# A graph kernel's step re-ordered: transposes side by side, block sums one step later, node stages in a PSUM bank of their own

## The chip, the cores and the metric

The kernel runs on one NeuronCore of a Trainium2 chip. The engines named here are TensorE (PE, with its weight loads as PEld), VectorE (DVE), ScalarE (ACT), GpSimd (POOL) and SyncE (SP, which only issues transfers). Each engine works through its own queue in the order of the program. The metric is the device time of one launch in microseconds; less is better.

## What is computed

Two layers of a graph network on 6,250 nodes with 256 features and 106,250 edges, sorted by the node they point to, all in float32. In the reference, cut to what matters:

```python
# layer 0
msg = relu(x[src] + edge_attr)
agg = segment_sum(msg, dst, num_segments=N)
h = x + (x + agg)
f = gelu(bn1(h) @ W1.T + b1) @ W2.T + b2
x1 = layernorm(x + bn2(h + f))
# layer 1
m = gelu((x1[src] + edge_attr) @ W1m + b1m) @ W2m + b2m
agg = segment_sum(m, dst, num_segments=N) / maximum(deg, 1)
u = gelu(agg @ W1u + b1u) @ W2u + b2u
out = layernorm(x1 + layer_norm(x1 + u, gamma, beta))
```

## The kernel before

Edges come in tiles of 128, eight tiles to a *span*: 831 tiles make V = 104 spans, the last of 7 tiles with 10 edges in its last. A span has two groups of four tiles (`g` = 0 and 1), and a group two pairs (`q` = 0 and 2). Nodes come in 25 blocks of 256 rows, the last (block 24) of 106. There is one pass over all spans for each layer (`step_0` and `step_1`).

The edges being sorted, the targets of a span lie in a window of some 160 nodes, and those of two neighbouring tiles in 32 slots. So the segment sum is two products with 0/1 matrices: `into_slots` (L855) sums a span's rows into 4 x 32 slots with one-hots that `one_hots` makes (L833); the result is copied out by ScalarE (L861); `into_blocks` (L879) adds the slots into the accumulator of one or two node blocks, with a mask of the span's window made by `slot_nodes` (L842), or a wider one where a block is begun (L873). In pass 0 a third product (L886) adds up the degrees.

A span's rows of `x[src]` (or, in pass 1, of `proj[src]`, which is x1 @ W1m + b1m) are fetched by `gather` (L772): one indirect transfer a tile, 128 rows of 1 KB, issued by GpSimd into one of five ring buffers. A ring is free again when `into_slots` of the span five earlier has read it. Loads of edge features (L760, L1158) are issued by SyncE three steps ahead into eight buffers.

The product edge_attr @ W1m is needed in pass 1, but half of it (group 0) is made in pass 0, stored to memory (`zst`, L1041) and loaded in pass 1, so that TensorE has like work in both. For a pair of tiles, `turned` transposes the features (four transposes, L785, into one PSUM bank of the pool eaP), ScalarE copies the result out (L790), and `product` multiplies with W1m (L798). Where no product is needed, `lifted` has ScalarE copy the features to PSUM (L809). `add_to_gathered` (L816, VectorE) adds the PSUM tile onto the ring, and `activated` (L824, ScalarE) applies Relu or Gelu over four tiles.

Step v gathers span v, adds and activates span u = v - 1, and sums span w = v - 2 into slots and blocks. When a block's last span has been summed, a Python generator (`nodes_0` or `nodes_1`) does the node work in stages, one a step, with `advance`; the stages lie in the list `running`. `nodes_0` has five: scale and copy the accumulator (L924, L929); W1 and Gelu (L935, L940); W2, residual and the first layer norm, up to the store of x1 (L948 to L962); transposes of x1 (L970, L973); the product with W1m and the store of proj (L979, L987). `nodes_1` has five as well: mean (L1086 to L1090); two with half of the first product each (L1100, L1105, L1109); the second product with the inner layer norm (L1115 to L1136); the outer one and the store (L1141). `normalized` makes statistics (L898, L899) on VectorE, a square root on ScalarE (L900, which loads another function table than Gelu) and the scaling on VectorE (L901, L905), all in one stage.

After pass 0 the last steps are drained, `join_weights` multiplies W2m with W1u (L1061 to L1080), and pass 1 begins. Its gathers need all of `proj`.

The schedule is written by hand (`tc.manual_schedule`): the order of the calls in a step is the order on each engine. PSUM has eight banks: two accumulators (accP), one for slot sums (slotP), one for transposes (eaP) and four (workP) that all other PSUM tiles take in turn. A tile that takes a bank waits until the tile before it in that bank has been read.

Of the kernel before, what the change touches and what calls it, by code (L numbers as in the profile page):

```python
# [14 lines left out]
P = 128  # L15
D = 256
KC = D // P
G = 4
# [484 lines left out]
def kernel(  # L503
# [224 lines left out]
    with (  # L728
# [6 lines left out]
        tc.tile_pool(name="eaP", bufs=1, space=bass.MemoryType.PSUM) as pse,  # L735
# [10 lines left out]
        def work():  # L746
            return psw.tile([P, 2, D], F32, name="workP")

# [30 lines left out]
        def turned(v, g, q, ea):  # L779

            pair = tiles_of(v, g)[q : q + 2]
            pe = pse.tile([P, 2, KC, P], F32, name="eaP")
# [64 lines left out]
        def into_slots(v, width):  # L847
# [3 lines left out]
            ps = pss.tile([P, D + 1], F32, name="slotP")  # L851
# [8 lines left out]
            sums[v] = hp.tile([P, D + 1], F32, name="sums")  # L860
            nc.scalar.copy(sums[v][:, :width], ps[:, :width])  # L861

        def into_blocks(v, acc, opened, degs=None):

            its, hot, lo0 = sums.pop(v), hot2s.pop(v), window[v][0]
            for b, lo, hi in parts(v):
# [17 lines left out]
                if degs is not None:  # L884
                    ps = work()
                    nc.tensor.matmul(  # L886
                        ps[:1, 0, : hi - lo], lhsT=its[:, D : D + 1], rhs=at,
                        start=True, stop=True,
                    )
                    nc.vector.tensor_add(degs[b][:, cols], degs[b][:, cols], ps[:1, 0, : hi - lo])  # L890
# [21 lines left out]
        def advance():  # L912

            for gen in list(running):
                if next(gen, "done") == "done":
                    running.remove(gen)


        def nodes_0(b, acc, xb, deg):
# [11 lines left out]
            ps = work()  # L931
# [12 lines left out]
            ps = work()  # L944
# [14 lines left out]
            nc.vector.tensor_add(ps, ps, bn2_b[:n, None, :].to_broadcast([n, H, D]))  # L959
            x1 = npool.tile([P, SH, D], F32, name="x1")  # L960
            normalized(x1, ps, n, H)
# [3 lines left out]

            x1T = npool.tile([P, KC, SB], F32, name="x1T")
            ps = work()
# [8 lines left out]
            ps = work()  # L976
# [23 lines left out]
        def opened_0(b):  # L1000
# [10 lines left out]
            degs[b] = npool.tile([1, SB], F32, name="degs", bufs=3)  # L1011
            nc.vector.memset(degs[b], 0.0)
            return False

        def step_0(v):
            u, w = v - 1, v - 2
            if v + AHEAD < V:
                load_0(v + AHEAD)
            if v < V:
                gather(v, x)  # L1020
                first = turned(v, 0, 0, eas[v, 0])
                z = ep.tile([P, G, D], F32, name="z", bufs=2)
            if 0 <= w:
                slot_nodes(w)
            if 0 <= u < V:
                for q in (0, 2):
                    add_to_gathered(u, 0, q, lifted(u, 0, q, eas[u, 0]))
            if 0 <= w:
                into_slots(w, D + 1)
            if v < V:  # L1030
                second = turned(v, 0, 2, eas[v, 0])
                nc.vector.tensor_copy(z[:, 0:2, :], product(*first))  # L1032
            if 0 <= u < V:
                activated(u, 0, AF.Relu)
                for q in range(0, len(tiles_of(u, 1)), 2):
                    add_to_gathered(u, 1, q, lifted(u, 1, q, eas[u, 1]))
                one_hots(u)
            full = into_blocks(w, acc, opened_0, degs) if 0 <= w else []
            if v < V:
                nc.vector.tensor_copy(z[:, 2:4, :], product(*second))  # L1040
                nc.sync.dma_start(out=zst[v], in_=z.rearrange("p j d -> p (j d)"))  # L1041
            if 0 <= u < V:
                activated(u, 1, AF.Relu)
            advance()
            for b in full:
                gen = nodes_0(b, acc.pop(b), xbs.pop(b), degs.pop(b))
                next(gen)
                running.append(gen)
# [33 lines left out]
        def nodes_1(b, acc, x1, deg):  # L1082
# [13 lines left out]
            for i in range(0, UC, 2):  # L1096
                ps = work()
# [6 lines left out]
                for o in (i, i + 1):  # L1104
# [3 lines left out]
                    )  # L1108
                    nc.scalar.activation(  # L1109
# [4 lines left out]
            ps = work()  # L1114
# [7 lines left out]
            ps = work()  # L1122
# [6 lines left out]
            nc.vector.tensor_add(ps[:n, :H, :], ps[:n, :H, :], r[:n, :H, :])  # L1129
            mv = normalized(None, ps, n, H)  # L1130
            for h in range(H):
                nc.vector.scalar_tensor_tensor(
                    ps[:n, h, :], ps[:n, h, :], mv[:n, h, 0:1], row["L1_gnn_gamma"][:n, :],
# [3 lines left out]
                    ps[:n, h, :], ps[:n, h, :], mv[:n, h, 1:2], y[:n, h, :],  # L1137
                    op0=ALU.mult, op1=ALU.add,
                )
            yield  # L1140
            normalized(y, ps, n, H)  # L1141
# [22 lines left out]

        def step_1(v):
            u, w = v - 1, v - 2
# [4 lines left out]
            if 0 <= w:  # L1171
                slot_nodes(w)
            some = 0 <= u < V
            if some:
                first = turned(u, 1, 0, eas[u, 1])
                for q in (0, 2):
                    add_to_gathered(u, 0, q, lifted(u, 0, q, eas[u, 0]))
            if 0 <= w:
                into_slots(w, D)
            if some:  # L1180
                second = turned(u, 1, 2, eas[u, 1])
                add_to_gathered(u, 1, 0, product(*first))
                activated(u, 0, AF.Gelu)
                one_hots(u)
            full = into_blocks(w, acc_1, opened_1) if 0 <= w else []
            if some:
                add_to_gathered(u, 1, 2, product(*second))
                activated(u, 1, AF.Gelu)
            advance()
            for b in full:  # L1190
                gen = nodes_1(b, acc_1.pop(b), x1s.pop(b), degs_1.pop(b))
                next(gen)
                running.append(gen)
# [3 lines left out]
        for v in range(V):  # L1197
            step_0(v)
        for v in range(AHEAD):
            load_1(v)  # L1200
        step_0(V)
        step_0(V + 1)
        join_weights()
        while running:
            advance()
        for v in range(V + 2):
# [64 lines left out]
```

## Time and profile before

| what | value |
|---|---|
| median of 10 runs | 2214.35 us (2212.11 to 2219.56) |
| the profiled execution | 2214.09 us |
| its span, first to last instruction | 2212.3 us |
| mean granted TensorE clock | 0.980 |
| TensorE busy, 550 to 1050 us (pass 0) | 450.3 of 500 us |
| TensorE busy, 1250 to 1700 us (pass 1) | 374.7 of 450 us |
| transfers, share of the 16 DMA engines, pass 0 / pass 1 | 0.88 / 0.70 |
| Sqrt's table loads (L900) | 73, 1.283 us each |

Pass 0 runs from about 35 to 1080 us of the span, pass 1 from about 1116 to 2160 us. The profile puts an engine's time down as busy only while an instruction works; what lies between two instructions, such as the issuing of a transfer, is not in it. A line of the timeline gives start, duration, engine, line, operation, and in brackets the idle time before it with the instruction that seems to have ended it. A wait that is put down to an instruction that had ended long before was another's.

### The profile page before, as it was taken

Reading aid. Unit: us, or ns where it says so; the run is one execution under the profiler, and the core shown is the slowest. Engines: PE = TensorE matmul, PEld = TensorE weight load, DVE = VectorE, ACT = ScalarE, POOL = GpSimd, SP = SyncE. Lnnn points to the kernel's source line nnn. Section 1 sums busy time; section 2 is a strip of 40 time slices with the busy share of each in tenths; the row PEclk is TensorE's granted clock in tenths of the full one; section 3 lists DMA queues with packets and bytes.
Section 4 is the critical chain, followed back from the end, with each engine's and each line's share of the span. In section 5 each row is a group of like instructions: output and inputs, shape, how many; then the busy total and the mean of one; then the engine's idle time right before and its main releaser. Section 6 shows DMA issues by size and latency. Waiting matters only on the chain.

```text
span 2212.3 us, 38426 instructions
## 1 busy us (share of the span) xinstructions
PE 1847.1 (83%) x11916; PEld 1444.5 (65%) x11916; DVE 1441.8 (65%) x4130; ACT 1347.7 (61%) x2143; POOL 1578.5 (71%) x1671
## 2 busy tenths in 40 slices
PE   3888998989889889889867878888888888888885
PEld 2667767767667667667646666666666666666664
DVE  4567667666666766666534676667667667667665
ACT  2566666667666666666534666666666566656664
POOL 3777777777777777777367777777777777777770
PEclk9999999999999999999979999999999999999997
DMA  7888889989889888888466777667667766776650
GB/s 230 266 275 285 281 270 293 280 273 291 279 272 291 277 280 285 282 272 280 158 195 214 223 231 233 213 212 242 213 224 230 232 213 220 236 231 213 223 179 16
DMA packets 313740, 531.79 MB, mean 240 GB/s; under 512 B 37989, under 2 KB 233144, under 8 KB 313400
## 3 DMA queue, kind: packets, MB, share of 16 engines
q1 hardware_dynamic: 231190, 307.82, 41.1%
q0 software_dynamic: 79744, 217.71, 33.6%
q10 hardware_dynamic: 2594, 3.71, 0.5%
q8 instruction: 100, 1.64, 0.3%
q14 instruction: 112, 0.92, 0.1%
HBM read 455.34 MB, written 73.75 MB: 239 GB/s over the span
## 4 chain that ended last, share of the span: by engine, by line
PE 46%; DVE 16%; DMA 15%; ACT 10%; issue 9%; POOL 4%; DVEq 0%; ACTq 0%; POOLq 0%
PE workP L798 22%; DMA ring<-in_x_dram,src_sb 9%; PE acc L879 5%; PE eaP L785 5%; DMA ring<-proj,src_sb 4%; PE workP L1100 4%; POOL ring L772 4%; DVE ring L816 3%; ACT ring L824 3%; PE slotP L855 2%; ACT eaT L790 2%; PE workP L948 2%; ACT uT L1109 2%; DVE hot L833 2%; DVE stats L898 2%
## 5 line engine op out<-in xcount | busy, mean ns | idle before, releaser
L772 POOL DMA_INDIRECT ring<-proj,src_sb x831 | 788.9, 949 | 292.8 <-issue 151.5
L772 POOL DMA_INDIRECT ring<-in_x_dram,src_sb x831 | 787.8, 948 | 286.2 <-issue 130.5
L816 DVE TENSOR_TENSOR ring<-workP,ring 128x512 f32<-128x512 f32 x832 | 546.3, 685 | 438.2 <-ACT workP L809 156.7
L798 PE MATMUL workP<-w1m_sb,eaT 128*128 128x256 f32 x3324 | 813.8, 389 | 7.7 <-DVE ring L816 6.6
L824 ACT ACTIVATE ring<-ring 128x1024 f32<-128x1024 f32 x418 | 439.5, 1052 | 561.1 <-DVE ring L816 482.1
L798 PEld LDWEIGHTS workP<-w1m_sb,eaT 128*128 128x128 f32 x3324 | 613.6, 194 | 100.8 <-DVE ring L816 17.6
L785 PE MATMUL eaP<-ident,ea 128*128 128x128 f32 x1662 | 265.0, 283 | 152.5 <-ACT eaT L790 152.5
L785 PEld LDWEIGHTS eaP<-ident,ea 128*128 128x128 f32 x1662 | 192.5, 143 | 265.1 <-ACT eaT L790 239.8
L809 ACT COPY workP<-ea 128x512 f32<-128x512 f32 x624 | 345.0, 589 | 0.0
L855 PE MATMUL slotP<-ring,hot 128*32 128x257 f32 (+1 forms) x3324 | 269.3, 388 | 68.6 <-ACT ring L824 46.4
L879 PE MATMUL acc<-hot,sums 128*128 128x160 f32 (+19 forms) x1360 | 225.1, 292 | 77.1 <-DVE hot L873 46.4
L790 ACT COPY eaT<-eaP 128x512 f32<-128x512 f32 x416 | 243.1, 584 | 58.0 <-PE eaP L785 56.9
L879 PEld LDWEIGHTS acc<-hot,sums 128*128 128x128 f32 x1360 | 200.8, 193 | 106.5 <-DVE hot L873 46.9
L833 DVE TENSOR_SCALAR hot<-ramp,slot 128x32 f32<-128x32 f32 x1662 | 267.3, 261 | 0.0
L855 PEld LDWEIGHTS slotP<-ring,hot 128*32 128x32 f32 x3324 | 110.1, 109 | 162.9 <-ACT ring L824 77.2
L1032 DVE COPY z<-workP 128x512 f32<-128x512 f32 x104 | 71.9, 691 | 85.3 <-PE workP L798 85.3
L900 ACT ACTIVATE mv<-mv,eps 128x2 f32<-128x2 f32 (+1 forms) x75 | 22.2, 295 | 140.3 <-DVE mv L899 140.0
L1100 PE MATMUL workP<-fT,w 128*128 128x256 f32 (+1 forms) x400 | 95.1, 382 | 0.1
L900 ACT ACT_TABLE_LOAD x73 | 93.7, 1283 | 1.3
L1125 PE MATMUL workP<-w2u_sb,uT 128*128 128x256 f32 (+1 forms) x392 | 90.2, 383 | 3.4 <-ACT uT L1109 3.4
L1125 PEld LDWEIGHTS workP<-w2u_sb,uT 128*128 128x128 f32 (+1 forms) x392 | 74.9, 192 | 14.2 <-ACT uT L1109 3.8
L1100 PEld LDWEIGHTS workP<-fT,w 128*128 128x128 f32 x400 | 76.7, 195 | 11.1 <-PE workP L1100 0.5
(109 smaller groups left out, 1421.0 us busy)
## 6 DMA issues: line engine op xcount, KB each, us to landing
ea<-in_edge_attr_dram SPq DMA_DIRECT2D x310, 512.0 KB
zst<-z SPq DMA_DIRECT2D x104, 512.0 KB
ea<-zst SPq DMA_DIRECT2D x104, 512.0 KB
ring<-in_x_dram,src_sb POOLq DMA_INDIRECT x831
ring<-proj,src_sb POOLq DMA_INDIRECT x831
xb<-in_x_dram SPq DMA_DIRECT2D x24, 256.0 KB
x1d<-x SPq DMA_DIRECT2D x24, 256.0 KB
proj<-y SPq DMA_DIRECT2D x24, 256.0 KB
```

The lines of the kernel that those rows point to most:

```text
L772: nc.gpsimd.indirect_dma_start(out=rings[v % RING][:n, g * G + j, :D], out_offset=None, in_=table, in_offset=bass.IndirectOffsetOnAxis(ap= ...
L785: nc.tensor.transpose(pe[:, j, k, :n], ea[:n, q + j, k * P : (k + 1) * P], ident[:n, :n])
L790: nc.scalar.copy(eaT[:, j:k, :, :n], pe[:, j:k, :, :n])
L798: nc.tensor.matmul(ph[:n, j, :], lhsT=eaT[:, j, k, :n], rhs=w1m_sb[:, k, :], start=(k == 0), stop=(k == KC - 1),)
L809: nc.scalar.copy(ps[:n, j:k, :], of[:n, q + j : q + k, :])
L816: nc.vector.tensor_add(r[:n, at + j : at + k, :D], ps[:n, j:k, :], r[:n, at + j : at + k, :D])
L824: nc.scalar.activation(at, at, func)
L833: nc.vector.tensor_scalar(hots[v][:n, j, :], ramp[:n, :SLOTS], slot[:n, t : t + 1], None, op0=ALU.is_equal,)
L855: nc.tensor.matmul(ps[q * SLOTS : (q + 1) * SLOTS, :width], lhsT=hot[:n, j, :], rhs=r[:n, j, :width], start=(i == 0), stop=(i == PAIR - 1 ...
L879: nc.tensor.matmul(acc[b][:, k, cols], lhsT=its[:, k * P : (k + 1) * P], rhs=at, start=(begins and k == 0), stop=(last_span[b] == v and k ...
L1100: nc.tensor.matmul(ps[:, o - i, :width], lhsT=w12[:, k, o * P : (o + 1) * P], rhs=mT[:, k, :width], start=(k == 0), stop=(k == KC - 1),)
L1125: nc.tensor.matmul(ps[:n, h, :], lhsT=uT[:, k, h * P : h * P + n], rhs=w2u_sb[:, k, :], start=(k == 0), stop=(k == UC - 1),)
```

## The change

- The bank of eaP becomes `nodeP`, which all stages of `nodes_0` and `nodes_1` use, one after the other (`node_work`). Transposes take workP, so that workP holds transposes, lifted features and products only, in turn.
- In a step, both pairs are transposed at the start, then the one-hots are made, the block sums of span v - 3 (not v - 2) follow, then adds, a node stage, a product, the slot sums of v - 2, the other product.
- `activated` of the second group moves to the next step, ahead of the slot sums that read it.
- The first generator of `running` advances in mid-step, the others at its end. One more step drains each pass.
- `normalized` is taken apart (`deviations`, `inverted`, `scaled`), with a stage's end between the statistics and the root. `nodes_0` has six stages now, `nodes_1` seven. Some intermediate results move from PSUM to SBUF tiles, so that a stage's bank is read within the stage.
- The degrees come from one product a span, into the free columns of the slot bank.
- `join_weights` runs after step 0 of pass 0.

```diff
-        tc.tile_pool(name="eaP", bufs=1, space=bass.MemoryType.PSUM) as pse,
+        tc.tile_pool(name="nodeP", bufs=1, space=bass.MemoryType.PSUM) as psn,
...
+        def node_work():
+            return psn.tile([P, 2, D], F32, name="nodeP")
...
-            pe = pse.tile([P, 2, KC, P], F32, name="eaP")
+            pe = work().rearrange("p j (k e) -> p j k e", k=KC)
...
+            if degs is not None:
+
+                span = window[v][1] - lo0
+                nc.tensor.matmul(
+                    rest[:, :span], lhsT=its[:, D : D + 1], rhs=hot[:, :span], start=True, stop=True
+                )
+                for b, lo, hi in parts(v):
+                    to = degs[b][:, lo - b * SB : hi - b * SB]
+                    nc.vector.tensor_add(to, to, rest[:, lo - lo0 : hi - lo0])
...
-        def advance():
-
-            for gen in list(running):
+        def advance(which):
+
+            for gen in which:
                 if next(gen, "done") == "done":
                     running.remove(gen)
+
+        def finish():
+            while running:
+                advance(list(running))
+
+        def deviations(of, n, H):
+
+            stats = npool.tile([P, SH, 6], F32, name="stats")
+            mv = npool.tile([P, SH, 2], F32, name="mv", bufs=3)
+            for h in range(H):
+                nc.vector.bn_stats(stats[:n, h, :], of[:n, h, :])
+                nc.vector.bn_aggr(mv[:n, h, :], stats[:n, h, :])
+            return mv
...
         def step_1(v):
-            u, w = v - 1, v - 2
+            u, w, full = v - 1, v - 2, v - 3
             if v + AHEAD < V:
                 load_1(v + AHEAD)
             if v < V:
                 gather(v, proj)
-            if 0 <= w:
-                slot_nodes(w)
             some = 0 <= u < V
             if some:
                 first = turned(u, 1, 0, eas[u, 1])
-                for q in (0, 2):
-                    add_to_gathered(u, 0, q, lifted(u, 0, q, eas[u, 0]))
-            if 0 <= w:
-                into_slots(w, D)
+                second = turned(u, 1, 2, eas[u, 1])
+                one_hots(u)
+            early, late = running[:1], running[1:]
+            if 0 <= full:
+                full_1(full)
+            if 0 <= w < V:
+                activated(w, 1, AF.Gelu)
             if some:
-                second = turned(u, 1, 2, eas[u, 1])
+                add_to_gathered(u, 0, 0, lifted(u, 0, 0, eas[u, 0]))
+                add_to_gathered(u, 0, 2, lifted(u, 0, 2, eas[u, 0]))
+            advance(early)
+            if some:
                 add_to_gathered(u, 1, 0, product(*first))
                 activated(u, 0, AF.Gelu)
-                one_hots(u)
-            full = into_blocks(w, acc_1, opened_1) if 0 <= w else []
+            if 0 <= w < V:
+                slot_nodes(w)
+                kept_slots(w, into_slots(w, D))
             if some:
                 add_to_gathered(u, 1, 2, product(*second))
-                activated(u, 1, AF.Gelu)
-            advance()
-            for b in full:
-                gen = nodes_1(b, acc_1.pop(b), x1s.pop(b), degs_1.pop(b))
-                next(gen)
-                running.append(gen)
+            advance(late)
...
         for v in range(V):
             step_0(v)
+            if v == 0:
+                join_weights()
         for v in range(AHEAD):
             load_1(v)
-        step_0(V)
-        step_0(V + 1)
-        join_weights()
-        while running:
-            advance()
-        for v in range(V + 2):
+        for v in range(V, V + 3):
+            step_0(v)
+        finish()
+        for v in range(V + 3):
             step_1(v)
-        while running:
-            advance()
+        finish()
```

`kept_slots` is the copy L861, `full_1` calls `into_blocks` and begins a block's generator; `step_0` is re-ordered in the same way, with its two transposed pairs of span v at the start and the products' copies to `z` where `step_1` has adds.

## The prediction

> **What bounds the kernel now.** The page shows TensorE busiest (83%) and its chain gives TensorE 46%, so the first reading is that idle time on TensorE is worth money. I checked that with the history of the line that issues gathers (L772), then with the timeline of GpSimd's queue.
>
> ```profile
> PE 1847.1 (83%) x11916; PEld 1444.5 (65%) x11916; DVE 1441.8 (65%) x4130; ACT 1347.7 (61%) x2143; POOL 1578.5 (71%) x1671
> L772 POOL DMA_INDIRECT ring<-in_x_dram,src_sb x831: 880/947/1137, 35.6 to 1075.5; - x167
> L772 POOL DMA_INDIRECT ring<-proj,src_sb x831: 877/947/1099, 1115.8 to 2157.2; - x167
> 1074.26 0.95 POOL L772 DMA_INDIRECT ring<-in_x_dram,src_sb  x1 [0.30 <-PE workP L798]
> 1075.51 0.88 POOL L772 DMA_INDIRECT ring<-in_x_dram,src_sb  x1 [0.30 <-DVE hot L842]
> 1115.81 0.98 POOL L772 DMA_INDIRECT ring<-proj,src_sb  x1 [39.42 <-DMA proj<-y]
> 1117.10 0.94 POOL L772 DMA_INDIRECT ring<-proj,src_sb  x1 [0.30 <-issue]
> ```
>
> Two lines give 831 gathers with first and last start. (1075.5 - 35.6)/830 = 1.2529 us a gather in pass 0 and (2157.2 - 1115.8)/830 = 1.2547 in pass 1. The timeline shows what 1.25 is made of: 0.95 of work and a gap of 0.30 that is the same whoever is named as releaser, and the same from 37 us on, in the first step, where the other engines have little to do. So GpSimd is saturated in both passes, and 71% "busy" is 100% of its queue. Going through the gathers of both passes I found one gap beyond 0.32 after the first gather of a pass: 0.68 us at 1546. The time is therefore 35.6 (to the first gather) + 1041 + 39.4 (the turn between the passes) + 1042 + 54 (2158.1 to the end, 2212.3). A step of eight gathers is 10.03 us, and an order that spares TensorE time inside a step buys nothing there. Only the turn, the tail and the prologue can move, or a gather that begins to wait.
>
> Next: how far the computing lags. I took each step's copy of the slot sums (L861, one a step) against the issue of the last gather of its span. In pass 0 the lag is 8 to 13 us and does not grow: the sums follow the gathers. In pass 1 it is 8 us at span 3, 13 at 30, 17 at 60, 21 at 102. So in pass 1 computing takes about 0.12 us a step more than gathering, and ends some 12 us late. This shows in the tail:
>
> ```profile
> 2157.20 0.88 POOL L772 DMA_INDIRECT ring<-proj,src_sb  x1 [0.30 <-issue]
> 2170.45 0.37 ACT L861 COPY sums<-slotP 128x256 f32<-128x256 f32 x1
> 2174.14 0.40 DVE L816 TENSOR_TENSOR ring<-workP,ring 10x256 f32<-10x256 f32 x1
> 2205.10 0.54 DVE L905 TENSOR_SCALAR y<-workP,mv 106x256 f32<-106x256 f32 x1
> PE eaP L785 <- ACT eaT L790: 64.1, 74, 1.4
> PE acc L879 <- DVE hot L873: 33.3, 19, 1.8
> PE slotP L855 <- ACT ring L824: 21.1, 24, 0.9
> PE acc L879 <- DVE hot L842: 18.4, 12, 1.7
> 1100.00:1105.00 5.00, 4.51 (x16) 3.47 (x17) 1.55 (x4) 3.21 (x5) 0.00 (x0) 0.66 0.17 56
> 2181.00:2188.00 7.00, 6.92 (x21) 5.48 (x21) 2.33 (x7) 0.91 (x2) 0.00 (x0) 0.60 0.01 2
> ```
>
> The last gather is issued at 2157.2 and landed at 2159.3 (the chain's transfer of 2.13), yet its rows are added at 2174.1. The four waits are TensorE's from 1300 to 2100, 137 us or 1.7 a step, and its busy time there is about 8.3 a step. The last two lines are windows; their column before the last two is the granted clock.
>
> **The change, part by part.** *Steady steps.* Both pairs' transposes come together into two workP banks, so the copy that the second pair waited for (64 us) lies behind transposes and block sums; the window masks (L842) and one-hots are made a step earlier than the block sums that read them (52 us); the late Gelu of the second half is done before the products (21 us). TensorE's step falls from 10.15 towards 8.3 plus little, below 10.03. Value in the steady steps: 0, since GpSimd's queue covers it; without that cover the 1.7 would count, up to 104 x 1.7 = 177 us a pass. What it buys is the lag: pass 1 ends up to 12 us earlier in its adds. Queues: SP's loads wait for the same buffers, freed at the same place in a step, 3 steps ahead, and the z, x1 and proj stores stay behind them; GpSimd's queue is the same list in the same order. A ring is freed later (the slot sums move behind the first product, L798's 8 instructions = 1.9, the node stage, up to 3, and a step's relu): some 6 us. A gather of span v needs the slot sums of v-5, which 32 gathers (40 us) cover; the lag of 21 now leaves 19 of it, less 6 is 13 spare. Cost 0; each us beyond would be a us.
>
> *Other moves.* The separate mask product for the degrees (L886) becomes one a step instead of one a block: less work, covered. join_weights goes from the turn into step 0; its 7.9 us (1085.9 to 1093.8, L1061 to L1080) hide there, since GpSimd fills four more rings before it needs the first: 40 us, and span 0's sums came at 53 against 85.7 needed.
>
> *The turn.* Both kernels start from the last landing, about 1077.7. Before, y of the last row block is ready at 1109.3. After: adds done 1078.9, mask L842 0.3, block 23's sums (L879) 0.7, bias-scale L924 1.0, relu 0.9; the slot sums of 103 (L855, 14 of them, 1.75) begin 0.5 before the relu ends, copy 0.4, with hand-overs 1083.7; block sums of 103 1.0, y of block 22 (L979) 2.0, its add 0.7, since one nodeP bank lets the next product in only then: 1087.5, against 1084.3 for the same product L935 before. L935 2.0, Gelu 0.9: the products of x1 (L948) start at 1090.5, against 1093.6, join_weights being gone. From there two blocks share the bank: 2.9 + adds 1.5 + first product of block 24 1.0 + Gelu 0.6 + table load 1.3 + Sqrt 0.3 + scale 1.2 = 1099.8; its two adds 1.0, transposes 0.8, copy 0.6, L979 2.2, add 0.7, transposes 0.4, copy 0.4, L979 1.1, add 0.4, with hand-overs: 1108.2. That is -1.1. But TensorE idles some 4.5 us before 1079.3, and the window row shows 0.66 of the clock after 3.1 idle: 4 us of such products would cost 1 to 2.5. Bounds -1.1 and +1.5; I take 0, between.
>
> *The tail.* With the lag gone the 128x512 add ends at 2159.7, mask L842 at 2160.0, the last add at 2160.4, 14 us earlier. But the path behind it grows: block sums come one step later, and nodes_1 has seven stages for five, in one bank. At rates of undisturbed rows: block sums of 102 1.1, the 16 products of block 22 (L1125) 3.5, its add 0.7, statistics 1.2, mask 0.3, reciprocal and mean of block 24 1.5 = 2168.5 (slot sums of 103 beneath). Four L1132/L1136 2.05, statistics 1.2, L1105 0.9, Gelu 0.9, table load and Sqrt 1.6, scale 1.2, L1105 0.9 = 2177.7. Block 24: L1100 1.05, L1105 0.6, Gelu 0.6, copy 0.6, two adds 1.4, L1100 1.05, L1105 0.6 = 2183.7. Block 23: L1125 3.5, add 0.7, statistics 1.2, Sqrt with its load waiting, 4 x 0.5 = 2192.5; block 24's L1125 1.05, add, statistics 1.1, block 23's scale 1.2, then 1.2 + 0.6 + 1.1 = 2198.8, with 0.05 to 0.1 at each of some 25 hand-overs 2200.4. Before: 2205.6. So -5.2. At the clock of the second window row (0.60 after 4.7 us idle; L1100 365 ns each for 217) L1125 takes 5.8 for 3.5, and the waits for the one bank leave TensorE idle 3 to 5 us before most products: +2.3, +1.2, 2 x 0.7, +1, +1 = +6.2 makes +1.0. Bounds -5.2 and +1.0. The gaps resemble those ahead of the slow rows, but not all are as long: I take -2.3.
>
> [...]
>
> *Sum:* 0 + 0 - 2.3 = -2.3 us. The profiled execution took 2214.09 (span 2212.3 and 1.8 around it); it lies 0.26 under the median of ten, 2214.35. On the median: **2212.0**.
>
> **Rivals.**
> A. The ends gain in full: the clock stays up since work arrives evenly. For it: 2188 to 2195 is at 1.00 again with gaps in it. Against: the one bank. -1.1 - 5.2 = -6.3: 2208.0.
> B. Slower: the longer end path without the gain in lag. If steps of pass 1 stay above 10.03 us (ScalarE's and VectorE's queues in order, with node stages put between the adds), adds end at 2174.5 as now and 40.0 us follow (2160.4 to 2200.4) where 31.1 did: +8.9, 2223. It decides from a lag 5.2 us above the gathers. Against: TensorE 8.3, VectorE 305/45 = 6.8, ScalarE 6.2 a step, all with room.
> C. The gathers begin to wait for rings: needs 13 us more lag, 0.12 a step beyond today; then every further us counts. Against: as B.
> D. The reorder does what it says and TensorE's page line falls, with no change in time: that is the forecast itself.
>
> **How the numbers follow.** About 0.2% (4.4 us) is what this measurement can tell from no change. Forecast (-4.4 to +4.4) 0.58. A and what lies near it, 0.30; B with C, 0.12. The range: from just below A, 2207, to 2218, which takes in both upper bounds (+2.5, 2216.9) and the mild part of B.
>
> **What would show it.** Gathers again 1.25 us apart, first at 35.6; L772's pass 1 beginning within 2 us of 1115.8; waits of transposes for the eaT copy nearly gone; lag of the slot sums in pass 1 flat; the last add within 3 us of 2160.4; in the tail a low granted clock and products waiting for nodeP's readers. Wrong if GpSimd shows gaps over 0.3, if the lag still grows, or if the spacing of gathers itself changes.

## The result, and the profile after

The changed kernel takes 2227.26 us (median of 9 runs, 2219.73 to 2230.24), the kernel before beside it 2215.89: a ratio of 1.0043, 95% interval 1.0031 to 1.0054. It became slower by 0.4%, where "no change in time" was forecast and 2218 was the upper end of the range. The profiled execution after took 2233.02 us, with a span of 2231.2 against 2212.3 before: 18.9 us are to be found. It was the slowest of the eleven executions of the changed kernel; between the medians lie only 11.4 us, so the terms below are those of this execution and not of a typical one. In two of the five groups of runs below the kernel before itself took 2816 us (late_loads, warm_turn, drain_banks, join_back) and 2785 us (after_again, warm_both, before_join0, best2) instead of some 2216, for a reason that stays open, so ratios are always to the kernel before of the same group.

The two groups of gathers in the view of one line (durations min/median/max, then first and last start), after:

```profile
L775 POOL DMA_INDIRECT ring<-in_x_dram,src_sb x831: 881/947/1139, 35.8 to 1075.6; - x167
L775 POOL DMA_INDIRECT ring<-proj,src_sb x831: 877/947/1212, 1131.7 to 2174.7; - x167
```

Pass 0 lies where it was (35.8 to 1075.6; 35.6 to 1075.5 before). Pass 1 begins at 1131.7 instead of 1115.8 and lasts 1043.0 instead of 1041.4. From its last gather to the end of the span it is 56.5 us, 55.1 before. So of the 18.9 us, 15.8 were lost at the turn, 1.6 in pass 1, 1.4 in the tail and 0.1 ahead of the turn. GpSimd's timeline shows the turn as its one gap:

```profile
1075.63 0.88 POOL L775 DMA_INDIRECT ring<-in_x_dram,src_sb  x1 [0.30 <-issue]
1131.71 0.98 POOL L775 DMA_INDIRECT ring<-proj,src_sb  x1 [55.20 <-DMA proj<-y]
```

The wait is 55.20 us, 39.42 before; the 0.30 between gathers is as it was (first line).

The steady steps did what the change says. In the view of waits between 1300 and 2100 us (total, times, longest), TensorE's transposes no longer wait for the eaT copy (64.1 us before; products wait 13.3 for it now). What stands at the top of all engines is VectorE waiting for gathers; of TensorE's own waits these two are the longest:

```profile
DVE ring L819 <- DMA ring<-proj,src_sb: 117.8, 99, 2.8
PE acc L886 <- DVE hot L880: 38.8, 19, 3.1
PE acc L886 <- DVE hot L845: 34.7, 22, 3.4
```

The computing keeps up with the gathers: the lag of the slot sums in pass 1, start of a span's last gather to start of the copy of its sums, no longer grows. Its mean over the first 26 spans is 11.6 us and over the last 26 it is 11.4, where before it was 11.9 and 19.7. The last rows are added at once, and yet the end comes no sooner (VectorE's timeline in the tail, after):

```profile
2177.99 0.41 DVE L819 TENSOR_TENSOR ring<-workP,ring 10x256 f32<-10x256 f32 x1 [0.75 <-PE workP L801]
2224.51 0.41 DVE L947 TENSOR_SCALAR y<-y,mv 106x256 f32<-106x256 f32 x1
```

The last add ends 3.7 us after the issue of the last gather (17.3 before), but from there to the end of the last scaling it is 46.5 us (31.1 before). Both ends, turn and tail, can be cut at the same marks, which the experiments use throughout:

| us | before | after |
|---|---|---|
| issue of the last gather of pass 0 to the end of its last add | 4.1 | 8.6 |
| from there to the end of the last y (the add before the store of proj) | 29.7 | 41.2 |
| from there to the first gather of pass 1 | 6.5 | 6.2 |
| issue of the last gather of pass 1 to the end of its last add | 17.3 | 3.7 |
| from there to the end of the last scaling | 31.1 | 46.5 |

*The late landing.* The chain of waits around the turn names the transfer that ends last, after and then before (start, duration):

```profile
1074.38 8.74 DMA ring<-in_x_dram,src_sb
```

```profile
1074.26 3.43 DMA ring<-in_x_dram,src_sb
```

SyncE's queue has the reason. After (first fence), the first loads of pass 1 are issued at 1072.3, since the store of z that stands in front of them had left; before (second fence), that store leaves only at 1075.04:

```profile
1072.29 0.43 SPq L1204 DMA_DIRECT2D xb<-x1d  x1
1073.70 0.43 SPq L1211 DMA_DIRECT2D ea<-zst  x1
1074.23 0.44 SPq L763 DMA_DIRECT2D ea<-in_edge_attr_dram  x1
```

```profile
1075.04 0.32 SPq L1041 DMA_DIRECT2D zst<-z  x1
1075.41 1.81 SPq L1151 DMA_DIRECT2D xb<-x1d  x1
```

*The clock.* Windows of the turn after, then one of before (PE, PEld, DVE, ACT, POOL busy, granted clock, share of the transfers, GB/s):

```profile
1080.00:1085.00 5.00, 0.39 (x2) 0.42 (x3) 1.62 (x5) 0.92 (x2) 0.00 (x0) 0.50 1.06 382
1085.00:1090.00 5.00, 5.00 (x22) 2.53 (x21) 1.15 (x4) 2.42 (x5) 0.00 (x0) 0.50 0.66 230
1090.00:1095.00 5.00, 4.41 (x17) 2.56 (x17) 0.24 (x1) 0.38 (x1) 0.00 (x0) 0.50 0.00 0
1100.00:1105.00 5.00, 4.07 (x10) 2.73 (x10) 0.00 (x0) 0.84 (x2) 0.00 (x0) 0.50 0.15 51
```

```profile
1095.00:1100.00 5.00, 2.37 (x18) 2.09 (x16) 2.88 (x8) 0.72 (x2) 0.00 (x0) 1.00 0.00 0
```

TensorE waits 9.65 us for the last landing, and then the granted clock stays at 0.50 to 1105, though TensorE is busy for most of that time; before, it was 1.00 until 1100. A clock of 0.50 is called cold below. What half a clock makes of the path is in TensorE's timeline:

```profile
1084.61 2.01 PE L886 MATMUL acc<-hot,sums 128*128 128x50 f32 x8 [9.65 <-DVE hot L845]
1093.38 3.78 PE L1015 MATMUL nodeP<-w1m_sb,fT 128*128 128x256 f32 x8
1099.10 3.78 PE L969 MATMUL nodeP<-fT,w1t_sb 128*128 128x256 f32 x8 [1.93 <-DVE y L1019]
1110.92 1.24 PE L969 MATMUL nodeP<-fT,w1t_sb 128*128 128x106 f32 x8 [2.02 <-DVE x L994]
1118.57 3.67 PE L1015 MATMUL nodeP<-w1m_sb,fT 128*128 128x256 f32 x8 [0.68 <-ACT fT L1009]
```

The eight instructions of L1015 take 3.78 here and 1.97 before (L979). The waits of 1.93 and 2.02 for VectorE are those for the one nodeP bank. The same is seen in the tail:

```profile
2188.61 3.75 PE L1146 MATMUL nodeP<-fT,w 128*128 128x256 f32 x8 [3.17 <-DVE y L1187]
2204.97 6.60 PE L1173 MATMUL nodeP<-w2u_sb,uT 128*128 128x256 f32 x16 [0.74 <-DVE uT L1151]
2216.61 3.72 PE L1173 MATMUL nodeP<-w2u_sb,uT 128*106 128x256 f32 x8 [5.04 <-DVE y L1187]
```

### The profile page after: what moved, and what is told of

It reads as the page before. It is cut to its first block, busy times and chain, and to the rows that moved or that the text cites. A ratio compares the mean times of both kernels' runs of the same rounds, so it can differ in the third digit from the quotient of the medians.

```text
span 2231.2 us, 37619 instructions
## 1 busy us (share of the span) xinstructions
PE 1885.8 (85%) x11784; PEld 1443.8 (65%) x11784; DVE 1421.3 (64%) x4130; ACT 1342.9 (60%) x2139; POOL 1580.5 (71%) x1671
## 3 DMA queue, kind: packets, MB, share of 16 engines
q0 software_dynamic: 79744, 217.71, 33.1%
## 4 chain that ended last, share of the span: by engine, by line
PE 21%; DMA 14%; DVE 7%; issue 6%; POOL 3%; ACT 3%; DVEq 0%; POOLq 0%; ACTq 0%
DMA ring<-proj,src_sb 13%; PE workP L801 9%; POOL ring L775 3%; PE acc L886 3%; PE slotP L858 3%; PE nodeP L1173 2%; DVE ring L819 2%; PE nodeP L1146 2%; DVE hot L836 1%; PE workP L788 1%; ACT ring L827 1%; DVE nodeP L1183 1%; PE nodeP L1015 1%; DVE y L1187 1%; ACT eaT L793 1%
## 5 line engine op out<-in xcount | busy, mean ns | idle before, releaser
L801 PE MATMUL workP<-w1m_sb,eaT 128*128 128x256 f32 x3324 | 842.5, 398 | 22.2 <-ACT eaT L793 16.8
L793 ACT COPY eaT<-workP 128x512 f32<-128x512 f32 x416 | 224.2, 585 | 211.7 <-PE workP L788 210.8
L788 PE MATMUL workP<-ident,ea 128*128 128x128 f32 x1662 | 222.8, 276 | 17.9 <-DVE ring L819 17.8
L858 PE MATMUL slotP<-ring,hot 128*32 128x257 f32 (+1 forms) x3324 | 231.6, 392 | 0.8 <-PE slotP L894 0.6
L788 PEld LDWEIGHTS workP<-ident,ea 128*128 128x128 f32 x1662 | 195.9, 143 | 45.6 <-DVE ring L819 22.8
L867 ACT COPY sums<-slotP 128x257 f32<-128x257 f32 (+1 forms) x208 | 75.6, 364 | 146.8 <-PE slotP L858 146.3
L1146 PE MATMUL nodeP<-fT,w 128*128 128x256 f32 (+1 forms) x400 | 104.4, 408 | 43.6 <-DVE y L1187 38.7
L1156 ACT ACTIVATE uT<-uT,cols_sb 128x256 f32<-128x256 f32 (+1 forms) x100 | 44.9, 495 | 141.7 <-DVE uT L1151 141.7
L1146 PEld LDWEIGHTS nodeP<-fT,w 128*128 128x128 f32 x400 | 79.5, 206 | 63.1 <-DVE y L1187 42.3
L1173 PE MATMUL nodeP<-w2u_sb,uT 128*128 128x256 f32 (+1 forms) x392 | 98.0, 407 | 5.8 <-DVE y L1187 5.0
```

The lines of the kernel that those rows point to most:

```text
L788: nc.tensor.transpose(pe[:, j, k, :n], ea[:n, q + j, k * P : (k + 1) * P], ident[:n, :n])
L793: nc.scalar.copy(eaT[:, j:k, :, :n], pe[:, j:k, :, :n])
L801: nc.tensor.matmul(ph[:n, j, :], lhsT=eaT[:, j, k, :n], rhs=w1m_sb[:, k, :], start=(k == 0), stop=(k == KC - 1),)
L858: nc.tensor.matmul(ps[q * SLOTS : (q + 1) * SLOTS, :width], lhsT=hot[:n, j, :], rhs=r[:n, j, :width], start=(i == 0), stop=(i == PAIR - 1 ...
L1146: nc.tensor.matmul(ps[:, o - i, :width], lhsT=w12[:, k, o * P : (o + 1) * P], rhs=mT[:, k, :width], start=(k == 0), stop=(k == KC - 1),)
L1173: nc.tensor.matmul(ps[:n, h, :], lhsT=uT[:, k, h * P : h * P + n], rhs=w2u_sb[:, k, :], start=(k == 0), stop=(k == UC - 1),)
```

## The experiments

Three causes were set against each other; the expectations number them as theories: the late landing (1, the collision), TensorE's cold clock (2), and the single bank (3).

**The loads of pass 1 later.**

```diff
-        for v in range(AHEAD):
-            load_1(v)
-        for v in range(V, V + 3):
-            step_0(v)
+        step_0(V)
+        step_0(V + 1)
+        for v in range(AHEAD):
+            load_1(v)
+        step_0(V + 2)
         finish()
```

> The changed kernel with the loads of pass 1 that SyncE issues at 1072 to 1079 moved behind the second draining step. Theory 1 (collision: these loads share the DMA engines with the last gathers, whose last landing took 8.74 us instead of 3.43): the last add of pass 0 comes some 5 us earlier (about 1079 instead of 1083.2), TensorE's idle time before it shrinks from 9.65 to about 4.5 us, the turn from 55.2 to between 46 and 50, the time to 2218 to 2222. Theory 2 (TensorE's clock alone): the landing is as late as now or its moving buys only itself; the stretch from the last add to the last y stays at 42 us, because 4.5 us idle still cool the clock: turn 50, time 2222. Theory 3 (the path through the draining steps is longer for its waits): landing irrelevant to the 42 us, as theory 2. If the loads were no cause: no change from 2227.

> The same kernel as late_loads (loads of pass 1 issued behind the second draining step), measured again because in the first measurement even the kernel before took 2816 us, with gathers that waited for ring buffers in every step, so that the landing of the last gathers said nothing. Where the kernel before takes some 2216 us: collision theory: last add of pass 0 at +4 us after the last gather's issue instead of +8.6, and the time 3 to 6 below the changed kernel's 2227; no part in it: +8.6 and 2227. The stretch from the last add to the last y (41.2) is left by both.

> The changed kernel as it is, beside late_loads_3 on one chip. Where the kernel before takes some 2216: ratio 1.0043 as before, last add at +8.6 after the issue of the last gather.

> The changed kernel with the loads of pass 1 behind the second draining step. If the late landing is a cost in every run: 4 to 6 us below after_again_2, ratio 1.0015 to 1.0025. If the profiler or chance made it, or if what is won there is lost again to later transfers: within 2 us of it.

late_loads (beside 2816 us): ratio 1.0229 (1.0194 to 1.0264); its last add came 30.7 us after the last gather, where gathers waited for rings all along, which tells nothing of the landing. late_loads_2: last add at +2.8 instead of +8.6; ratio 1.0029 (1.0014 to 1.0044), not apart from the changed kernel's. So both were measured on one chip: after_again_2 2225.82 us, ratio 1.0044 (1.0028 to 1.0061), last add at +8.3; late_loads_3 2221.26 us, ratio 1.0022 (1.0011 to 1.0033), last add at +2.7. That is 4.6 us between the medians for an edit that only moves loads, though the two intervals overlap. The chain of late_loads_3 has the transfer back near its old length:

```profile
1071.85 3.76 DMA ring<-in_x_dram,src_sb
```

What follows: the collision is real. The last add comes 5.6 and 5.8 us sooner behind the gather; in time it is 4.6 us by the pair on one chip and some 3 by the ratio of late_loads_2 against the changed kernel's. The stretch from the last add to the last y stayed long (39.9 and 35.0), as the other causes want it.

**The node stages of the draining steps in four banks.**

```diff
+        draining = []
+
         def node_work():
+            if draining:
+                return work()
             return psn.tile([P, 2, D], F32, name="nodeP")
...
         for v in range(V, V + 3):
             step_0(v)
+            draining.append(v)
         finish()
+        draining.clear()
         for v in range(V + 3):
             step_1(v)
+            if v >= V:
+                draining.append(v)
         finish()
```

> The changed kernel, with the node stages of the draining steps taking the four banks in turn instead of their single one. Theory 3 (the single bank): turn 55.2 falls by about 4 (its waits of 1.93 and 2.02 and the product of block 23 that waits for the add of block 22), the tail 56.5 by 5 to 11 (three waits of 3.0 to 5.0 us for readers of the bank), and the time by 9 or more. Theory 2 (cold clock): the order of arrival is not the bank's, the clock stays at 0.50 and each end gains under 2 us. Theory 1: no gain at the turn.

> The same kernel as drain_banks, measured again for the same reason. In the first measurement its stretch from the last add to the last y was 24.1 us, against 35.5 to 40.0 in the three others, and the stretch from the last add to the last scaling at the very end 32.6 against 46.6 to 46.8. Theory 3 (the single bank): these repeat, so where the kernel before takes 2216 the turn falls from 55 to about 39 and the tail from 56.5 to about 43: time 2227 - 16 - 14 = 2197, some 0.8% under the kernel before. Theory 2 (clock first): the clock stays at 0.50 and each end gains 2 to 5: 2217 to 2223.

Ratio 0.9946 (0.9929 to 0.9962), 2206.56 us (drain_banks_2); drain_banks, beside 2816 us, 1.0086 (1.0055 to 1.0116), where three kernels with the single bank had 1.0213 to 1.0243. Last add to last y 29.9 us instead of 41.2, last add to last scaling 32.9 instead of 46.5; the landing is as late as after (+9.0). Theory 3 had 2197; the order of size holds, and the bank alone, with what it does to the clock, turns a loss of 0.4% into a gain of 0.5%. But its turn still shows the clock at 0.50 from 1080 to 1100: the bank is not all.

**Extra products that nobody reads (filler), to keep the clock up.**

```diff
+        def fill(count):
+            idle = work()
+            for i in range(count):
+                nc.tensor.matmul(
+                    idle[:, i % 2, :], lhsT=w1m_sb[:, 0, :P], rhs=w1m_sb[:, 1, :],
+                    start=True, stop=True,
+                )
...
                 kept_slots(w, into_slots(w, D + 1))
+            if v == V:
+                fill(18)
```

> The changed kernel with 18 extra products into a tile that nobody reads, put into TensorE's queue in the first draining step behind the slot sums of span 102, about 8.5 us of work in the 9.65 us in which TensorE waits for the last gathers. Theory 2 (cold clock): the granted clock stays near 1.00 after 1085, the 42.3 us from the last add to the last y fall to 30 to 34, the turn from 55.2 to about 45, the time by 8 to 12 us, to 2216 to 2219. Theory 1 (collision alone): the landing stays at 1083, and the path gains under 2 us. Theory 3 (waits of the path, not rates): gain under 3 us, since the waits for one bank remain.

> The changed kernel with extra products that nobody reads: 18 (8.5 us) in the wait for the last gathers at the turn, and at the end 5, 5 and 9 in the waits of 3.2, 3.0 and 5.0 us for the single bank. Bank, order and loads are as in the changed kernel. If the cold clock is a cost of its own: the granted clock stays near 1.00; the stretch from the last add to the last y falls from 41.2 to about 30.5 (the prediction's path at full rate), the stretch from the last add to the last scaling from 46.5 to 40.0 (the prediction's warm sum); time 2227 - 10 - 6 = 2211. If the waits of the single bank are all there is: 41 and 46 stay, or fall by less than 3. If the clock matters but the path at full rate was sized too short: 33 to 37 and 41 to 44.

Beside 2816 and 2785 us: ratios 1.0213 (1.0186 to 1.0241) and 1.0045 (1.0014 to 1.0075), the changed kernel itself 1.0063 beside the second. At the turn they tell little: 18 products took 8.04 us in warm_turn and ended after the landing, which there left a shorter wait, so that they held up the path themselves; last y came 35.5 and 40.6 after the last add, 37.2 in after_again. The tail of warm_both is plain: 39.3 us from the last add to the last scaling instead of 45.8 in after_again, with bank and order untouched. The clock is then 6.5 us of the tail.

> The changed kernel as it is, on the same chip as the next three, so that their terms can be compared. Every theory: about 2227, 0.4% above the kernel before; last add of pass 0 at +8.6 us after the issue of the last gather, last y 41 after it, tail 56.

after_again: 2803.78 us beside 2785, ratio 1.0063 (1.0042 to 1.0085).

**Landing and clock mended, the single bank kept.** late_loads with fill(8) at the turn; in the tail, as in warm_both, filler ahead of the products that wait for the bank:

```diff
             for i in range(0, UC, 2):
+                if (b, i) in ((blocks - 2, 0), (blocks - 1, 2)):
+                    fill(5)
                 ps = node_work()
...
             yield
+            if b == blocks - 1:
+                fill(9)
             ps = node_work()
             for h in range(H):
                 for k in range(UC):
```

> The changed kernel, single bank and order untouched, with the loads of pass 1 behind the second draining step, 8 extra products (3.6 us) in the wait for the last gathers, and 5, 5 and 9 in the waits for the bank at the end. Cold clock as a cost of its own: last add at +3, last y 30 us after it (39.9 with cold clock in late_loads_2), last scaling 39 to 40 after the last add (39.3 in warm_both): against the profile of the changed kernel -5.8 -11 -6.5, so about 2207, which is what the prediction's rival A (both ends at full rate) had: 2208. Waits of the single bank alone: 38 to 40 and 45, time 2219 to 2222. The prediction's warm path too short by the waits: 34 to 36 and 40, 2212 to 2214.

2211.3 us, ratio 0.9968 (0.9956 to 0.998): the order of steps as changed, with the single bank, is then 0.3% faster than the kernel before. Last scaling 39.0 after the last add, as in warm_both: the 16 products that took 6.60 us in the tail of the changed kernel (L1173) take 3.69 here, and the mean granted clock from the last add to the last scaling is 0.96 for 0.67.

```profile
2192.73 3.69 PE L1187 MATMUL nodeP<-w2u_sb,uT 128*128 128x256 f32 x16 [0.74 <-DVE uT L1163]
```

The turn did less than hoped: 34.9 us, no better than late_loads_3 without the filler (35.0), since the clock fell again behind the bank's first wait of 1.93 us, in both. late_loads_3, TensorE's timeline:

```profile
1085.37 1.99 PE L1015 MATMUL nodeP<-w1m_sb,fT 128*128 128x256 f32 x8
1089.30 3.66 PE L969 MATMUL nodeP<-fT,w1t_sb 128*128 128x256 f32 x8 [1.93 <-DVE y L1019]
```

L1015 ran at full rate; after 1.93 us of waiting, L969 ran at half.

**Four banks, late loads, with and without filler.** banks_late joins the first two edits, best2 adds to it the filler at the turn, best the second edit as well:

```diff
                 kept_slots(w, into_slots(w, D + 1))
+            if v == V:
+                fill(8)
...
             yield
+            if b == blocks - 2:
+                fill(6)
             ps = node_work()
```

(the second of the two edits, at block 23's second product, is best's alone).

> drain_banks with the loads of pass 1 behind the second draining step, 8 extra products (3.6 us) ahead of the wait for the last gathers and 6 (2.7 us) ahead of the second product of block 23 at the end, to keep TensorE's clock up. If bank, collision and clock each have a part: 4 to 5 us (landing) and 2 to 4 us (clock) below drain_banks: about 2190. If the bank alone matters: as drain_banks. If the extra products get into the way: above it.

> best without its 6 extra products in the tail: node stages in four banks while draining, loads of pass 1 behind the second draining step, 8 extra products at the turn. In best the stretch from the last add to the last scaling was 34.3 against 32.9 in drain_banks_2, so the products in the tail were in the way: then 33 here and a time 1 to 2 below best (0.991 of the kernel before), ratio 0.990. If the difference was chance: the same ratio as best.

> best2 without its 8 extra products at the turn. Clock as a cost of its own: the wait before the last landing (some 4 us) still lets the clock fall, so last y 27 to 30 after the last add (29.9 in drain_banks_2, 22.9 in best): 4 to 7 us above best2. If an idle time of 4 us is too short for that: as best2, within 2 us.

> best2 measured again beside the others (four banks while draining, late loads, 8 extra products at the turn). Where the kernel before takes 2216: last add +3, last y 23 after it, tail 42 as in drain_banks_2: about 2197, ratio 0.990 to 0.992, and 7 + 6.5 below late_warm if the single bank costs 7 us each end at full clock, about level with late_warm if the bank matters only through the clock.

best 0.9910 (0.9893 to 0.9926); best2 0.9951 (0.9924 to 0.9978), beside 2785 us; banks_late 0.9896 (0.9880 to 0.9912), 2195.47 us; best2_2 0.9884 (0.9869 to 0.9900), 2192.35 us. best2 beats both kernels. Against banks_late the filler gave 4.4 us at the turn in the profiles (last add to last y 28.0 and 23.6) and 3.1 in the medians, with intervals that overlap. That the six products in the tail were in the way fits (34.3 in best, 31.5 in best2_2) and was not tried by itself. best2_2 at the turn:

```profile
1085.97 1.99 PE L1027 MATMUL workP<-w1m_sb,fT 128*128 128x256 f32 x8
1087.80 1.89 PE L981 MATMUL workP<-fT,w1t_sb 128*128 128x256 f32 x8
1093.39 1.04 PE L981 MATMUL workP<-fT,w1t_sb 128*128 128x106 f32 x8
1098.81 1.99 PE L1027 MATMUL workP<-w1m_sb,fT 128*128 128x256 f32 x8 [0.68 <-ACT fT L1021]
```

These are the lines L1015 and L969 of the changed kernel: no waits for VectorE's readers, full rate.

**The joining of the weights.** join_back puts join_weights back behind the second draining step of the changed kernel (in a tile of its own); before_join0 moves it to step 0 in the kernel before:

```diff
         for v in range(V):
             step_0(v)
+            if v == 0:
+                join_weights()
...
         step_0(V + 1)
-        join_weights()
```

> The changed kernel with the joining of the weights back at its old place behind the second draining step (in a tile of its own). If its removal from the turn is what let the clock fall: TensorE shows a granted clock near 1.00 after it, the stretch from the last add to the last y is 42 less 10 plus at most 8, so 36 to 40, and the time falls by 2 to 6 us. If the long idle time before it (9.65 us, from the late landing) is the cause: the joining itself runs at half clock and lengthens the path, +4 to +10 us, time 2231 to 2237. If the clock does not matter: +5 to +8.

> The kernel before with one part of the change alone: the joining of the weights in step 0 instead of the turn. If the joining's 7.9 us were on the path: turn 40.3 less 3 to 8, time down to 2209 to 2213. If it kept TensorE's clock up while TensorE waited: the clock falls to 0.5 to 0.66 in the turn, the products after it take up to twice as long, and the turn stays within 2 us of 40.3 or grows.

> before_join0 measured again. On the first chip its ratio was 0.9984 (0.9967 to 1.0002) and the stretch from the last add to the last y 23.0 us, with a granted clock of 1.00 up to it, against 29.7 in the kernel before. If the joining was on the path: 23 to 24 again, time 5 to 7 below the kernel before (ratio 0.997). If that was the other chip's: 28 to 30, ratio 1.000.

join_back (beside 2816 us): 1.0243 (1.0217 to 1.0268), stretch 40.0, where the changed order in late_loads and warm_turn had 36.0 and 35.5: no gain from putting it back. before_join0 (beside 2785 us): 0.9984 (0.9967 to 1.0002), stretch 23.0; before_join0_2: 2207.93 us, 0.9956 (0.9941 to 0.9970), stretch 22.2 instead of 29.7. Its windows of the turn:

```profile
1080.00:1085.00 5.00, 4.42 (x26) 2.33 (x22) 1.95 (x7) 2.03 (x4) 0.00 (x0) 1.00 1.03 380
1085.00:1090.00 5.00, 3.76 (x24) 3.37 (x24) 1.86 (x4) 2.78 (x5) 0.00 (x0) 1.00 0.72 253
```

So the joining's move is a gain of 7.5 us at the turn, and it was not what kept the clock up before. (The medians differ by 10.5 us, more than the turn explains; the rest was not looked into.)

**Do the steady steps have room?** One tile's product of every step of pass 1 is made twice:

```diff
-        def product(pair, eaT):
+        def product(pair, eaT, again=0):
...
-            for j, n in enumerate(pair):
+            for j, n in list(enumerate(pair))[:again] + list(enumerate(pair)):
...
-                add_to_gathered(u, 1, 2, product(*second))
+                add_to_gathered(u, 1, 2, product(*second, again=1))
```

> The changed kernel with one tile's product of every step of pass 1 made twice: two more logical products, about 0.95 us of TensorE, a step, some 98 us in all. The prediction said that the steady steps are worth nothing, since GpSimd's queue (10.03 us a step) covers TensorE's 8.3: then the time stays within 4 us of the changed kernel's 2227. If TensorE bounds the steps: up to 98 us more. If it is close to the bound, the lag of the slot sums grows in pass 1 and the last add comes later by that.

Ratio 1.0056 (1.0040 to 1.0073), against 1.0043: some 3 us, with intervals that overlap, for 61 us more of TensorE's busy time (1946.7 against 1885.8). In the profiles of both, TensorE's busy time from 1300 to 2100 us, after and then in cover:

```profile
1300.00:2100.00 800.00, 684.05 (x4293) 534.17 (x4292) 536.08 (x1558) 497.70 (x765) 606.16 (x637) 0.96 0.71 225
```

```profile
1300.00:2100.00 800.00, 729.27 (x4616) 582.05 (x4615) 537.76 (x1555) 497.94 (x764) 606.12 (x637) 0.99 0.73 225
```

TensorE is busy 45 us longer in these 800. At 0.95 us a step it would be 76; that the granted clock is 0.99 for 0.96 in these windows fits the difference. The lag is the same (mean 11.7 over the first 26 spans, 11.6 over the last 26), and the gathers of pass 1 lie within 1043.6 us: GpSimd's queue bounds the steps.

## Why the prediction was wrong

*What bounds it, steady steps, lag:* right. The gathers kept their spacing, the transposes' wait went, the lag in pass 1 is flat, and the last add comes 13.6 us sooner behind its gather (forecast 14). Rivals B and C fall: the lag did not stay, and in the profile of the changed kernel no gather waited for a ring (no gap over 0.32 us within a pass). That B's 2223 lies nearest to the 2227 is chance: its path, a lag that stays, did not happen.

*Queues:* wrong. "SP's loads wait for the same buffers, freed at the same place in a step" made the landing the same for both kernels, "about 1077.7". The store of z in front of the loads left some 3 us earlier, and the loads went in among the last gathers: landing 5.4 us later (1083.1 for 1077.7), priced at 0, worth 4.6 us in the pair on one chip.

*The turn's path at full rate:* right as far as it can be worked out; no run with the single bank kept the clock up through the whole turn. Between the last add and the last y TensorE has the same 19 groups of products in every version of the changed order. Their durations, summed, and the waits between them:

| | products | waits between | last add to last y |
|---|---|---|---|
| after | 32.4 | 9.2 | 41.2 |
| after_again_2 | 32.4 | 9.2 | 41.2 |
| late_loads_2 | 31.1 | 9.2 | 39.9 |
| late_loads_3, late_warm | 26.1, 26.1 | 9.2, 9.2 | 35.0, 34.9 |
| drain_banks_2 | 26.9 | 3.7 | 29.9 |
| banks_late | 24.7 | 4.0 | 28.0 |
| best2_2 | 19.3 | 4.1 | 23.6 |

At full rate the single bank's path is thus 41.2 - (32.4 - 19.3) = 28.1 us. The prediction's 1108.2 less 1078.9, its end of the adds, is 29.3. (The terms listed up to its 1099.8 make 1099.3; nothing hangs on that.) The kernel before needs 29.7 there, but 22.2 when the joining alone is moved (before_join0_2): at full rate the new order with its single bank is thus some 6 us longer, and the joining's 7.5 covered that.

*The turn's clock:* the step that failed. "4 us of such products would cost 1 to 2.5" was taken from one short cold stretch of the kernel before; it cost 13.1 us (32.4 - 19.3), and the working took 0. The late landing does not excuse it: with the landing back in place the same products still cost 11.8 and 6.8 us over full rate (late_loads_2 and late_loads_3). Two things were missed: after the wait for the landing the clock stayed low for much longer than 4 us of products (at 0.50 from 1080 to 1105 in the changed kernel), and it fell again behind a wait for the one bank of only 1.93 us (late_loads_3: L969 at 3.66 us, 1.89 in best2_2). The single bank was priced by its waits only, 9.2 - 4.1 = 5.1 us. By way of the clock it cost about as much again: with four banks the products take 5.5 us less in drain_banks_2 than after, and 6.8 less in best2_2 than in late_warm, at a like landing each (1.4 less in banks_late than in late_loads_3, whose first cold stretches differ).

The turn then adds up: landing +4.5 (8.6 for 4.1), path at full rate -1.6 (28.1 for 29.7, the joining's removal within it), clock +13.1, the rest -0.3: 15.7 of 15.8.

*The tail:* mechanism right, size wrong by the value taken. Its cold terms, 2.3, 1.2, 2 x 0.7, 1 and 1, make 6.9 and not the 6.2 written, so the upper bound should have been +1.7 and not +1.0 (the terms listed up to its 2177.7 also make some 0.3 less). On the warm path of 40.0 that is 46.9; the runs have 45.2 to 47.7 cold and 39.0 to 39.3 with filler. The value taken between the bounds, -2.3, was the mistake: +1.4 was measured, near the cold bound. With four banks the same stretch is 31.5 to 33.1, some 7 us below the 39.0, though its clock was lower than late_warm's (best2_2 0.86 for 0.96 in the mean): these are the waits of the single bank. The gain that the prediction saw in the lag is real; best2_2 needs 40.6 us from the last gather's issue to the end, 55.1 before.

Rival A, the ends in full, had 2208, and late_warm took 2211.3, but not by A's path: in its profile only the tail gained (48.8 us for 55.1), while the wait at the turn was 43.1 for 39.4. That the times agree is in part luck.

How long a cold stretch lasts differed from profile to profile. In banks_late the granted clock is 0.50 from 1079.95 to 1092, with TensorE busy for all but 0.6 us of it; in the changed kernel it is 0.50 from 1080 to 1105. But late_loads_3, after a like wait of 4.0 us, has it at 0.50 for only 3.4 us, and late_loads_2, the same kernel, for 13.65 (windows of late_loads_3, then of late_loads_2):

```profile
1079.22:1082.63 3.41, 3.41 (x17) 1.69 (x16) 1.15 (x4) 2.42 (x5) 0.00 (x0) 0.50 0.07 7
```

```profile
1078.71:1092.36 13.65, 11.60 (x42) 6.68 (x42) 2.70 (x9) 3.44 (x8) 0.00 (x0) 0.50 0.52 180
```

The one kernel's same products took 31.1 us in late_loads_2 and 26.1 in late_loads_3 between the last add and the last y. What makes the difference stays open.

## What to carry to other kernels

Where one queue saturates the steady steps, re-ordering them pays nothing there (here it bought only the lag, the last add 13.6 us sooner), and the prologue, turns and tail have to be costed by themselves, in the order in which the drain runs them and not at the rates of the steady state. A resource made single to free another (a bank here) was cheap while other work filled its waits (pass 1 lasted 1043.0 us for 1041.4); in the drain nothing filled them (9.2 us of waits between the last add and the last y, 4.1 with four banks in best2_2), and behind one of 1.93 us TensorE also took 3.66 us for products that take 1.89 (late_loads_3, best2_2). When an order lets a store leave earlier, look at what stands behind it in that queue and what it will collide with.

## What the runs showed of the hardware

- The granted clock fell right behind a wait of only 1.93 us (late_loads_3: L969 at 3.66 us, 1.89 in best2_2). After some 4 us idle it was at 0.50 for 3.4 us in late_loads_3, with TensorE busy throughout, for 13.65 in late_loads_2, with TensorE busy for 11.60 of them, and from 1079.95 to 1092 in banks_late, with TensorE busy for all but 0.6.
- The same kernel's products between the last add and the last y summed to 31.1 us in one profile and 26.1 in another (late_loads_2, late_loads_3).
- Loads of mostly 512 KB, issued from 2 us before the last two gathers on, lengthened a gather's transfer from 3.4 to 8.7 us, at a transfer share of 1.06 and 382 GB/s (window 1080 to 1085); with the loads moved it took 3.8.
